# Eight groups of a graph sum sorted by source, and 56 of its chunks summed inside the stage before it

## The chip, the core and the metric

The kernel runs on one core of a Trainium2 chip. The core has TensorE (PE, with its weight loads PEld), VectorE (DVE), ScalarE (ACT), GpSimd (POOL) and SyncE (SP), each with an instruction stream of its own, and 16 DMA engines. The metric is the device time of one execution in microseconds (us). A profiled execution is a run of its own; its trace is what all rows below come from.

## What is computed

A graph of 6250 nodes with 256 features and 106,250 directed edges (100,000 and one loop for each node), sorted by destination. Four blocks follow one another, each added to x: two sums over the edges with a network (512 wide), an attention over 64 slices for each of 8 heads, a normalised sum over the edges (the third sum), and a mixture of 8 experts with two chosen for each node.

```python
x = x + gin(layernorm(x), edges)          # first and second sum
x = x + slice_attention(layernorm(x))     # "desl" is its last step
h = layernorm(x) @ W                      # the third sum
out = segment_sum(h[src] * (dinv[src] * dinv[dst])[:, None], dst, N) + b
x = x + relu((out - mean) * rsqrt(var + eps) * gamma + beta)
x = x + experts(layernorm(x))
```

The third sum is taken before the product with W, which is the same: rows of layernorm(x) times dinv are written to a table, summed by destination, and multiplied by W afterwards.

## The kernel before

The nodes lie in 49 tiles of 128 rows (`NT`). The edges, in the order of their destinations, lie in chunks of 128; without the loops (`others`) there are 782. A chunk is summed in two steps. A gather on GpSimd's queue (`gather`, L162) fetches the 128 rows of a table that the chunk's sources name: an indirect DMA, 1536 bytes a row, three bf16 parts of 256. Then TensorE multiplies them by a one-hot matrix of the destinations (`multiply`, L183, three matmuls, one for each part) into PSUM. VectorE makes the one-hots, up to nine chunks in one instruction (`Sums.hot`, L227).

The destinations are cut into half-overlapping groups k = 0 to 96, each 128 nodes wide, 64 apart. Group k takes the fixed chunks `start(k)` to `start(k+1)`: twelve for k = 0, then eight each. Whether every chunk's destinations lie in its group's window is computed on the chip; if one doesn't, the sum is made zero and redone in a slow loop (`rest`), whose count `n_rest2` is zero for the inputs used here. `Sums.__call__` runs over the chunks of one tile (two groups): it issues gathers up to 14 messages ahead (the ring of buffers), multiplies chunk by chunk, and lets the caller put other work between (`between`). `add` puts a finished group's sum where it belongs: an even group on its tile, an odd one half on each of two.

The stages, in order:

- The first sum (from about 100 to 1125 us) with the first network behind it. Beside it the list of edges without loops is built (`lists`, L754 to L882): steps of VectorE on a 128-row buffer `big`, one handed out at each call of `between`. It writes sources and destinations to DRAM (`flat`) and reads them back in chunk order into `others.src` and `others.dst`, and it leaves the flag for `rest`.
- The second sum (about 1154 to 2145 us), with the second network and the first half of the attention.
- The small attention core (about 2185 to 2200 us), a chain of small steps on TensorE, VectorE and ScalarE that ends in the matrix `M`.
- The output stage (`desl`, L1313 to L1335, from 2200 us). For groups of four tiles: load the slice weights `swT`, four matmuls a tile with M into `po` (L1325, a PSUM tile for two tiles, four buffers), add to x (L1327), layer norm (`layer_norm`, L353 to L367), split in three bf16 parts (`split`, L372 to L376), write to the table T3 in DRAM (L1335, on ScalarE's queue). The order of instructions in this stage is made by a scheduler, engine by engine.
- `rest` for T3 (L1341), a loop that runs no time here.
- The third sum with the experts (from 2301 us): an order written by hand on all engines but GpSimd. For each tile t: SP loads (`load_ahead`, `load_experts`), the scaled own row is added (L1701), then `sums(t, between, 7)`. The seven calls of `between_products` put in the one-hots of the next tile, a piece of a `choice` chain (two tiles each: product with W, layer norm, gate, places), and pieces of expert blocks. `send` scatters the chosen rows to the experts' regions, also an indirect DMA on GpSimd's queue. A tail combines the experts' results.

Of the kernel before, what the change touches and what calls it, by code (L numbers as in the profile page):

```python
# [9 lines left out]
F32 = mybir.dt.float32  # L10
# [11 lines left out]
def gin_transolver_gcn_moe(ctx: ExitStack, tc: tile.TileContext, a: dict, out: bass.AP):  # L22
# [58 lines left out]
    all_edges, others = Chunks(E), Chunks(E - N)  # L81
    NCH2 = others.n
    QC2 = -(-NCH2 // P)
    assert (E, N) == (106250, 6250) and others.per == 16 and CPT == all_edges.per
# [93 lines left out]

    def multiply(pa, hot, msg, F, start, stop, ones=0):

        for s in (2, 0, 1):
            n = F + ones if s == 2 else F
            ins = nc.tensor.matmul(pa[:, :n], hot, msg[:, s * F:s * F + n], start=(start and s == 2),  # L183
                                   stop=(stop and s == 1))
        return ins

    class Sums:
# [4 lines left out]
        def __init__(self, edges, table, pool, depth, hots, ps, add, ones=0, whole=None, is_whole=lambda k: k % 3 == 1):  # L192
            self.whole, self.whole_at = whole, is_whole
            self.edges, self.start = edges, edges.start
            self.table, self.hots, self.ps, self.add, self.ones = table, hots, ps, add, ones
            W = table.shape[1]
            self.F = W // 3
            self.ring = [pool.tile([P, W + 4 * ones], BF16, name=f"msg{i}") for i in range(depth)]
            self.of = [None] * depth
            self.hotf = None  # L200
            self.n, self.made, self.beside = 0, {}, None
            self.early, self.each = False, None

        def is_whole(self, k):
            return self.whole is not None and self.whole_at(k)

        def message(self, c, k):
            i = c % len(self.ring)
            m, whole = self.ring[i], self.is_whole(k)
# [9 lines left out]
        def hot(self, k, c0):  # L219

            if (k, c0) not in self.made:
                n = min(HOTS, self.start(k + 1) - c0)
                if self.is_whole(k):
# [9 lines left out]
        def __call__(self, t, between=None, times=7):  # L233
# [4 lines left out]
            for k in ks:  # L238
                pa = self.ps.tile([P, 512], F32, name="pa", tag="agg", bufs=2)
                for c in range(self.start(k), self.start(k + 1)):  # L240
                    while self.n < min(c + len(self.ring), self.edges.n):
                        of = next(u for u in range(k, 2 * NT) if self.n < self.start(u + 1))
                        table = self.whole if self.is_whole(of) else self.table
                        ins = gather(self.message(self.n, of)[:, :table.shape[1]], table, self.edges.src[:, self.n:self.n + 1])
                        self.n += 1
                        if self.beside is not None:
                            in_order(ins)
                            self.beside(t)
                    c0 = c - (c - self.start(k)) % HOTS
                    hot, msg, ends = self.hot(k, c0)[:, c - c0, :], self.message(c, k), (c == self.start(k), c == self.start(k + 1) - 1)  # L250
                    if self.is_whole(k):
# [28 lines left out]

    def rest(table, add, n_of, count=None, begin=None, kept=None):


        n = nc.values_load(n_of[0:1, 0:1], min_val=0, max_val=NT)
        W = table.shape[1]
        with tc.tile_pool(name="rest", bufs=1) as w, tc.tile_pool(name="rest_ps", bufs=1, space=PSUM) as ps:
            with tc.For_i(0, n, 1) as t:
# [11 lines left out]
                with tc.For_i(c0, c1, 1) as c:  # L299
# [10 lines left out]
                    nc.vector.tensor_scalar(hot, node, k[:, 4:5], None, op0=OP.is_equal)  # L310
                    pa = ps.tile([P, 512], F32, name="pa")
                    if parts_ is F32:
# [135 lines left out]
    with tc.tile_pool(name="own", bufs=1) as own:  # L448
# [153 lines left out]
        with tc.tile_pool(name="g1w", bufs=1) as wp, \  # L602
# [151 lines left out]
            def lists():  # L754
# [77 lines left out]
                nc.sync.dma_start(flat[0], j_[:, :n])  # L832
                yield
                q, r = divmod(n, P)
                for i in range(2):
# [192 lines left out]
    core = {}  # L1028
    right, befores = ExitStack(), ExitStack()
    early = befores.enter_context(tc.tile_pool(name="pre", bufs=1, side="right"))  # L1030
    with tc.tile_pool(name="attn", bufs=1) as ap_:
        tok = ap_.tile([P, KG, D + 1], F32, name="tok")
# [189 lines left out]


        back = ExitStack()
        bw = back.enter_context(tc.tile_pool(name="desl", bufs=2))
# [86 lines left out]

        with back, tc.tile_pool(name="desl_ps", bufs=2, space=PSUM) as ps:  # L1313
            w = bw
            for ts in groups(4, 5):
                J = len(ts)
                x1 = xr[:, ts[0]:ts[-1] + 1, :]
                swT = w.tile([P, 4, HG], F32, name="swT", bufs=3)
                nc.sync.dma_start(swT[:, :J, :], tiles_of(SW, ts))
                for j0 in range(0, J, 2):  # L1320
                    js = range(j0, min(j0 + 2, J))
                    p = ps.tile([P, 2, D], F32, name="po", tag="mm", bufs=4)
                    for j in js:
# [9 lines left out]
                for _ in split(hr[:, :J], hs[:, :J, :], hs[:, :J, :], nc.vector.tensor_tensor):  # L1333
                    pass
                nc.scalar.dma_start(block(T3, ts), hr[:, :J].rearrange("p j s f -> p j (s f)"))  # L1335
    right.close()
    effs.close()


    nc.vector.tensor_scalar(ln3, ln3, own_times, None, op0=OP.mult)  # L1340
    rest(T3, add_to(lambda t: S3[ds(t, 1)].rearrange("o p f -> p (o f)"), D), n_rest2, kept=kept)  # L1341

    late = ctx.enter_context(ExitStack())
    late.enter_context(tc.manual_schedule(engines={mybir.EngineType.SP, mybir.EngineType.PE,
                                                   mybir.EngineType.Activation, mybir.EngineType.DVE}))
    msgs = late.enter_context(tc.tile_pool(name="g3msg", bufs=1))
    hots = late.enter_context(tc.tile_pool(name="g3hot", bufs=4))
    w = late.enter_context(tc.tile_pool(name="g3", bufs=2))
    ew = late.enter_context(tc.tile_pool(name="g3e", bufs=2))
    wxs = late.enter_context(tc.tile_pool(name="g3x", bufs=1))  # L1350
    ps = late.enter_context(tc.tile_pool(name="g3ps", bufs=2, space=PSUM))
    wx = wxs.tile([P, NE, EW], F32, name="wx")
    def add3(k, pa):
        t = k // 2
        if k % 2 == 0:
            return nc.vector.scalar_tensor_tensor(s3s[t], pa[:, :D], ln3[:, 1, t:t + 1], s3s[t],
                                                  op0=OP.add, op1=OP.add)
# [3 lines left out]
    start = others.start  # L1361
    sums = Sums(others, T3, msgs, 14, hots, ps, add3)
    sent = [[] for _ in parts]
# [178 lines left out]
    def load_experts(t):  # L1542

        for e in range(2 * t, min(2 * t + 2, NE)):
            n = KD * HID
# [124 lines left out]
    def between_products(t, k):  # L1670
        if k in (1, 4) and t + 1 < NT:
            of = 2 * t + 2 + k // 4
            if of <= 2 * NT - 2:
                sums.hot(of, start(of))
        if chains and next(chains[0], chains) is chains:
            chains.pop(0)
# [16 lines left out]
    for i, ts_ in enumerate(parts):  # L1693
        for q in range(0, len(ts_), TG):
            ts = ts_[q:q + TG]
            for t in ts:
                load_ahead(t)
                load_experts(t)
                s = s3s[t]

                nc.vector.scalar_tensor_tensor(s, xr[:, t, :], ln3[:, 0, t:t + 1], s, op0=OP.mult, op1=OP.add)  # L1701
                k = iter(range(SLOTS))
# [52 lines left out]
```

## Time and profile before

| | us |
|---|---|
| median of 10 runs (lowest, highest) | 3571.91 (3571.21, 3573.78) |
| profiled run, its own time | 3574.07 |
| its span | 3572.2 |
| POOL busy | 2505.2 (70%) |
| PE busy | 2836.3 (79%) |
| DVE busy | 1548.3 (43%) |
| ACT busy | 866.5 (24%) |

How to read the lines that follow: the slices cut the span into 40 parts of 89 us, and each digit is the busy share in tenths. A group line has the line of code, the engine, the operation, out<-in by the program's names, the count, then busy time and mean ns of one, then the idle time before it and what ended most of that. A timeline line has the start, the duration, engine, line, operation, out<-in, the shape and the count, and in brackets the idle time before and what ended it. "T" is whichever table is read or written, "msg" a message buffer. A matmul in float32 has two records in the trace. The granted clock is the share of TensorE's full speed.

### The profile page before, as it was taken

To read this page: it belongs to the slowest core of one execution; us is meant where nothing else is said; L and a number is where in the kernel's file an instruction comes from. 1 tells how busy PE (TensorE), PEld (TensorE's weight loads), DVE (VectorE), ACT (ScalarE), POOL (GpSimd) and SP (SyncE) were. 2 spreads that over 40 slices of the span, in tenths; PEclk is the share of its full clock that TensorE was granted. 3 is DMA by queue.
4 is the path that set the end of the run, shared out by engine and by line. 5 is a ranking of instruction groups with operands and counts; after the bars stand their busy time and mean duration, and the time that the engine had idled before them with its cause. 6 is when DMAs were issued, how large, how long until landed. Compare 5 with 4: busy or idle time off the path is not lost. (4 is left out here: it accounts for less than half of the span.)

```text
span 3572.2 us, 42390 instructions
## 1 busy us (share of the span) xinstructions
PE 2836.3 (79%) x12790; PEld 1710.9 (48%) x12854; DVE 1548.3 (43%) x3988; ACT 866.5 (24%) x1737; POOL 2505.2 (70%) x2618
## 2 busy tenths in 40 slices
PE   2777788877787899999999988666777777778984
PEld 1334444433345354455444545533555555556653
DVE  5464222222223345554555545634444444444453
ACT  4111111111113022222222223411222232323442
POOL 3787777777775777777777760177777777777765
PEclk6699999999999999999999998866888888889988
DMA  8668888888885999889988883665666666666655
GB/s 272 192 210 258 265 260 260 270 259 255 255 253 196 380 311 307 303 303 311 310 305 303 306 287 101 241 217 172 193 192 192 190 192 191 192 191 208 203 173 171
DMA packets 356497, 861.51 MB, mean 241 GB/s; under 512 B 60104, under 2 KB 158674, under 8 KB 356266
## 3 DMA queue, kind: packets, MB, share of 16 engines
q0 software_dynamic: 174688, 611.60, 55.1%
q1 hardware_dynamic: 175066, 237.50, 19.2%
q10 hardware_dynamic: 6512, 9.63, 0.8%
q8 instruction: 107, 1.75, 0.2%
q14 instruction: 124, 1.02, 0.1%
HBM read 691.29 MB, written 167.21 MB: 240 GB/s over the span
## 5 line engine op out<-in xcount | busy, mean ns | idle before, releaser
L162 POOL DMA_INDIRECT msg<-T,srcT x2059 | 1972.7, 958 | 822.1 <-issue 435.3
L183 PE MATMUL pa<-msg,hot 128*128 128x257 bf16 (+2 forms) x6114 | 1173.8, 318 | 520.1 <-DMA msg<-T,srcT 473.2
L183 PEld LDWEIGHTS <-hot 128*128 128x128 bf16 x6177 | 627.6, 103 | 1180.4 <-issue 881.0
L227 DVE SCALAR_TENSOR_TENSOR hot<-dstT,node 128x1024 bf16<-128x1024 f32 (+2 forms) x255 | 310.4, 1218 | 28.3 <-PE pa L183 16.6
L162 POOL DMA_INDIRECT msg<-T2f,srcT x256 | 242.9, 949 | 78.0 <-issue 30.8
L642 DVE TENSOR_TENSOR dinv<-dinv,pa 128x1 f32<-128x1 f32 x145 | 22.2, 153 | 535.0 <-PE pa L183 499.6
L253 PE MATMUL pa<-msg,hotf 128*128 128x512 f32 x512 | 244.2, 599 | 8.1 <-DMA msg<-T2f,srcT 7.6
L1585 PE MATMUL ph<-wx,xdT 128*128 x448 | 214.1, 600 | 11.1 <-DVE yd L1600 7.1
L1599 PE MATMUL py<-wx,hT 128*128 x896 | 213.6, 381 | 1.1 <-ACT hT L1594 1.1
L919 PE MATMUL p<-h1T,W1b 128*128 128x512 f32 (+2 forms) x480 | 208.7, 533 | 0.0
L928 PE MATMUL p<-W2a,h2T 128*128 128x512 f32 x392 | 206.7, 616 | 0.0
L1599 PEld LDWEIGHTS py<-wx,hT 128*128 128x128 f32 x896 | 168.7, 190 | 65.4 <-issue 42.8
L271 DVE SCALAR_TENSOR_TENSOR s<-s,own,pa 128x512 f32<-128x512 f32 x97 | 71.9, 741 | 183.0 <-PE pa L183 116.8
L1594 ACT ACTIVATE hT<-pt,wb 128x128 f32<-128x128 f32 x448 | 127.7, 368 | 44.7 <-PE pt L1591 42.4
L253 PEld LDWEIGHTS pa<-msg,hotf 128*128 128x128 f32 x512 | 91.3, 190 | 90.7 <-issue 53.4
L1359 DVE TENSOR_TENSOR s<-s,pa 64x256 f32<-64x256 f32 x96 | 40.2, 419 | 214.3 <-PE pa L183 212.8
L1472 POOL DMA_INDIRECT XD<-xn,place x98 | 97.6, 996 | 44.2 <-issue 31.1
L1600 DVE TENSOR_TENSOR yd<-py,wb 128x256 f32<-128x256 f32 x112 | 47.2, 422 | 182.4 <-PE py L1599 178.2
L162 POOL DMA_INDIRECT g<-XD,place x98 | 97.2, 992 | 40.9 <-issue 14.0
L389 ACT ACTIVATE sT<-pt 128x512 f32<-128x512 f32 (+1 forms) x25 | 14.7, 589 | 456.7 <-PE pt L387 456.7
L162 POOL DMA_INDIRECT msg<-T1f,srcT x80 | 85.6, 1071 | 56.0 <-DVE b1b L158 31.9
L1587 ACT ACTIVATE h<-ph 128x512 f32<-128x512 f32 x112 | 66.9, 597 | 217.0 <-PE ph L1585 217.0
(379 smaller groups left out, 3658.6 us busy)
## 6 DMA issues: line engine op xcount, KB each, us to landing
XD<-zeros SPq DMA_DIRECT2D x204, 256.0 KB
msg<-T,srcT POOLq DMA_INDIRECT x2059
T<-tp SPq DMA_DIRECT2D x49, 384.0 KB
wb<-WB SPq DMA_DIRECT2D x112, 130.0 KB
xd<-XD SPq DMA_DIRECT2D x112, 128.0 KB
XD<-yd SPq DMA_DIRECT2D x112, 128.0 KB
T2f<-tf SPq DMA_DIRECT2D x49, 256.0 KB
s<-T2f SPq DMA_DIRECT2D x23, 512.0 KB
```

Of the source, the lines that this page charges most:

```text
L162: return nc.gpsimd.indirect_dma_start(out=msg, out_offset=None, in_=table, in_offset=bass.IndirectOffsetOnAxis(ap=ix, axis=0))
L183: ins = nc.tensor.matmul(pa[:, :n], hot, msg[:, s * F:s * F + n], start=(start and s == 2), stop=(stop and s == 1))
L227: nc.vector.scalar_tensor_tensor(hot[:, :n, :], self.edges.dst[:, c0:c0 + n, None].to_broadcast([P, n, P]), float(k * HALF), node2[:, k % ...
L253: self.last = nc.tensor.matmul(pa[:, :n], hot, msg[:, :n], start=ends[0], stop=ends[1])
L271: return nc.vector.scalar_tensor_tensor(at, at, times[rows], pa[rows, :F], op0=OP.mult, op1=OP.add)
L919: nc.tensor.matmul(p[:, :T], W1b[:, k, m * P:(m + 1) * P], h1T[:, k, :T], start=(k == 0), stop=(k == KH - 1))
L928: nc.tensor.matmul(p, h2T[:, k, j * P:(j + 1) * P], W2a[:, k, :], start=(k == 0), stop=(k == KH - 1))
L1472: ins = nc.gpsimd.indirect_dma_start(out=XD[i], out_offset=bass.IndirectOffsetOnAxis(ap=place[:r, t, c:c + 1], axis=0), in_=xn[:r, j, :], ...
L1585: nc.tensor.matmul(p[:, :HID], xdT[:, k, :], W1[:, k, :], start=(k == 0), stop=(k == KD - 1))
L1587: nc.scalar.activation(h, p[:, :HID], AF.Copy)
L1594: nc.scalar.activation(hT[:, m, :], pt[:, m * P:(m + 1) * P], AF.Relu, bias=b1[:, m:m + 1])
L1599: nc.tensor.matmul(p[:, :D], hT[:, m, :], W2[:, m, :], start=(m == 0), stop=(m == KH - 1))
```

## The change

Eight groups (`EARLY`) are prepared. For each of the groups k = 0 to 7, its last eight chunks (`PER`; 1024 edges) are sorted by source on the chip, so that the first of the eight chunks names only rows at the front of the table T3, the second only rows further on, and so on. `LIMITS` says how many tiles of T3 each of the first seven may need: 12, 16, 24, 32, 36, 44, 46. The order of the edges inside a group does not matter to the sum.

- The sort is put into `lists`: after `flat` is written, rows of 1024 edges for the eight groups are read back onto 8 partitions, source and destination are packed in one number, 55 steps of a merging network of three VectorE instructions each order it, and the numbers are unpacked and written back. Edges out of the window or over a limit raise the flag for `rest`.
- The output stage now holds the third sum's buffers (messages, one-hots, PSUM). After the write of the group of four tiles that completes a limit, eight gathers are issued that read only the rows of T3 so far; after the next group's T3 write in program order their products are made, into sums `begun` in four PSUM banks. The buffers of `po` go from four to three. Eight one-hots (`look`) are made for it, 128 x 1024 each.
- The third sum leaves these 56 chunks out (`left`) and adds the eight begun sums at tile 0. The chains of `choice` begin at tile 4 instead of 2, and the experts' weights are loaded one tile later.
- The attention's pool goes to the other side of the memory, and `rest` takes a PSUM buffer from the stage's own pool.

The scheduler's order in the build of the changed kernel, on TensorE in the output stage: 90 output matmuls (L1325 before), 8 chunk products with 4 output matmuls between them, 11, 8 products with 4 between, 24, 8 with 4, 30, 8 with 4, 13, 8 with 4, 8, and then 16 products. On VectorE the eight one-hots stand between the steps of the attention core: one before and one after the first reciprocal, one after the four scalings of `tok`, one before the copy of `meanT`, two before that of `tokT`, one before that of `kT`, one before the maximum.

```diff
+    PER = others.per // 2
+    EARLY, ALIKE = 8, PER * P
+    LIMITS = [12, 16, 24, 32, 36, 44, 46]
+    def early_chunk(k, j):
+        return others.start(k + 1) - PER + j
...
+        def first_come(self, chunks):
+            self.ahead = {c: None for c in chunks}
+            self.order = chunks + [c for c in range(self.edges.n) if c not in self.ahead]
...
+        def left(self, k):
+            return [c for c in range(self.start(k), self.start(k + 1)) if c not in self.ahead]
...
+        def fetch_next(self, rows=None):
+            c = self.order[self.n]
...
+            ins = gather(self.message(c, of)[:, :table.shape[1]], table[:rows] if rows else table, self.edges.src[:, c:c + 1])
+            self.n += 1
...
+                nc.sync.dma_start(kd, rows_at(1))
+                nc.sync.dma_start(ks, rows_at(0))
...
+                nc.vector.scalar_tensor_tensor(key, ks, float(P), kd, op0=OP.mult, op1=OP.add)
+                m = 1
+                while m < ALIKE:
+                    k = m
+                    while k:
+                        yield
+                        if k == m:
+                            v = key.rearrange("r (b s t k) -> r b s t k", s=1, t=2, k=k)
+                        else:
+                            v = key.rearrange("r (b m) -> r b m", m=2 * m)[:, :, k:2 * m - k]
+                            v = v.rearrange("r b (s t k) -> r b s t k", t=2, k=k)
+                        lo_, hi_ = v[:, :, :, 0, :], v[:, :, :, 1, :]
...
+                        nc.vector.tensor_tensor(less, lo_, hi_, op=OP.min)
+                        nc.vector.tensor_tensor(hi_, lo_, hi_, op=OP.max)
+                        nc.vector.tensor_copy(lo_, less)
+                        k //= 2
+                    m *= 2
...
+                nc.sync.dma_start(rows_at(1), kd)
...
+                nc.sync.dma_start(rows_at(0), ks)
...
+        sums = Sums(others, T3, msgs, 14, hots, ps, None)
+        sums.first_come([early_chunk(k, j) for j in range(PER - 1) for k in range(EARLY)])
+        begun = [ps.tile([P, 512], F32, name="pa", tag=tag, bufs=2) for tag in ("agg", "agg", "tr", "tr")]
+        begun = [t[:, u * D:(u + 1) * D] for t in begun for u in range(2)]
...
+            def look(k):
+                hot_of[k] = w.tile([P, PER, P], BF16, name="ehot", bufs=EARLY)
+                c = early_chunk(k, 0)
+                nc.vector.scalar_tensor_tensor(
+                    hot_of[k], others.dst[:, c:c + PER, None].to_broadcast([P, PER, P]), float(k * HALF),
+                    node2[:, k % 2, None, :].to_broadcast([P, PER, P]), op0=OP.subtract, op1=OP.is_equal)
+            def products(n):
+                for k, j in to_add[:n]:
+                    ins = multiply(begun[k], hot_of[k][:, j, :], sums.message(early_chunk(k, j), k), D, j == 0 and k % 2 == 0,
+                                   j == PER - 2 and k % 2 == 1, after=heads.get((k - 1, j)) if k % 2 else None)
...
             for ts in groups(4, 5):
+                for k in range(EARLY):
+                    if ts[0] // 2 == k // 2 * 2:
+                        look(k)
...
-                    p = ps.tile([P, 2, D], F32, name="po", tag="mm", bufs=4)
+                    p = ps.tile([P, 2, D], F32, name="po", tag="mm", bufs=3)
...
                 nc.scalar.dma_start(block(T3, ts), hr[:, :J].rearrange("p j s f -> p j (s f)"))
+                products(len(to_add))
+                for j, limit in enumerate(LIMITS):
+                    if limit == ts[-1] + 1:
+                        for k in range(EARLY):
+                            sums.fetch_next(limit * P)
+                            to_add.append((k, j))
+            products(len(to_add))
...
-        if chains and next(chains[0], chains) is chains:
+        if t >= EARLY // 2 and chains and next(chains[0], chains) is chains:
...
-                load_experts(t)
-                s = s3s[t]
-                nc.vector.scalar_tensor_tensor(s, xr[:, t, :], ln3[:, 0, t:t + 1], s, op0=OP.mult, op1=OP.add)
+                load_experts(t - 1)
+                for u in range(EARLY // 2 + 1) if t == 0 else [t] if t > EARLY // 2 else []:
+                    nc.vector.scalar_tensor_tensor(s3s[u], xr[:, u, :], ln3[:, 0, u:u + 1], s3s[u], op0=OP.mult, op1=OP.add)
+                for u in range(EARLY) if t == 0 else []:
+                    add3(u, begun[u], True)
```

## The prediction

> **What bounds the kernel now.** I read the page's slices first, then busy time by stretches, then the waits, then the order of time around the change. GpSimd (POOL) is busy in every slice but two, around 2140 to 2320 us:
>
> ```profile
> POOL 3787777777775777777777760177777777777765
> L162 POOL DMA_INDIRECT msg<-T,srcT x2059 | 1972.7, 958 | 822.1 <-issue 435.3
> ```
>
> One gather holds POOL for 0.95 us and the next begins 0.30 us later: a pitch of 1.25. The stretches (length; then busy time and count of PE, PEld, DVE, ACT, POOL; granted clock, DMA share, GB/s) show 160 of them in 200 us of the third sum, with nothing between them, and 81 in 100 us of the first sum. The stage between them has none, and there PE is busy all of the time:
>
> ```profile
> 500.00:600.00 100.00, 79.95 (x370) 40.64 (x369) 27.03 (x49) 16.61 (x28) 75.62 (x81) 0.95 0.85 265
> ...
> 2201.00:2285.00 84.00, 84.00 (x390) 73.71 (x388) 64.85 (x171) 46.76 (x78) 0.00 (x0) 1.00 0.59 201
> ...
> 2320.00:2340.00 20.00, 13.92 (x57) 7.48 (x57) 5.60 (x9) 0.00 (x0) 15.12 (x16) 0.50 0.97 333
> ...
> 2600.00:2800.00 200.00, 151.99 (x861) 111.67 (x860) 93.58 (x357) 58.02 (x140) 151.55 (x160) 0.88 0.64 189
> ```
>
> From 2300 us on, POOL's own waits for TensorE never exceed its issue gap (137 waits, the longest 0.3 us):
>
> ```profile
> POOL msg L162 <- PE pa L183: 41.7, 137, 0.3
> ```
>
> So the first and third sums go at POOL's pitch, and the output stage between 2200.2 and 2298.3 us goes at PE's. Its end is the timeline to look at: the last write of T3, then a point that every engine passes (SP, which needs nothing of T3, starts its loads just then), then the first gather:
>
> ```profile
> 2298.29 0.33 ACTq L1335 DMA_DIRECT2D T<-hr  x1
> 2300.58 2.25 SPq L1376 DMA_DIRECT2D s<-S  x5
> 2301.37 0.94 POOL L162 DMA_INDIRECT msg<-T,srcT  x1 [161.44 <-issue]
> ```
>
> **Taken away after 2301 us.** 56 gathers leave a saturated queue: 56 x 1.25 = 70.0 us. Their 168 matmuls and eight one-hot instructions (1.22 us each, L227) lay beside POOL and give nothing. At the restart VectorE now has five scalings (0.55, L1701), eight additions of begun sums (0.43 to 0.87) and one hot before the first product, some 9 us behind SP's loads; the message ring of 14 covers 14 x 1.25 = 17.5 us, so I charge nothing. Without that cover it would be those 9. The first sends to the experts stand 38 gathers after the restart instead of 66, but as many behind their own tiles as before. SP's s3 load for tile 7 now waits for the first chain at tile 4, and the last four experts' loads queue behind it; no block needs them yet.
>
> **Core stage.** The build puts the eight one-hots of `look` into VectorE's queue between the steps of the small attention, a chain of VectorE and TensorE with waits of 0.3 to 1.9 us (the row of tokT: 1.94 idle before). Laying 1.22 us in each place: two ahead of the reciprocals and their product cost 2.4; one before meanT 0.99 beyond its wait, of which 0.5 shows because ScalarE makes the other half; two before tokT 0.5; one before kT 0.5; one before the maximum 0.3 to 0.4; the third one hides behind prow. M is ready 4.7 us later (bounds 2.4 to 9.8), at 2204.9.
>
> **Output stage, walked in the build's order.** An output matmul is 0.432 us (84.0 us for 390 half records, two each). TensorE's queue now reads: 90 output matmuls, eight chunk products (3 x 0.108 each) with four output matmuls between; 11, batch 2; 24, batch 3; 30, batch 4; 13, batch 5; 8, then batches 6 and 7 together. TensorE is in order, so a product that waits for its message holds every output matmul behind it, and through those VectorE's additions, ScalarE's layer norms, the T3 writes and the next batch's gathers.
> Prices: from a group's last matmul to its T3 write 11.4 to 14 us (2220.9 to 2232.4, 2227.9 to 2241.9); a 768 KB write lands 3.7 after its issue (bytes seen moving until 3.2 after 2284.45, and 0.5 for the semaphore); gather to product 3.2 to 3.9 after 3385.86, up to 6.9 at 2304 with DMA share 0.97; I take 3.9.
> Batch 1 in full: T3's third group was issued at 2232.4, now 2237.1; landed and first gather 2241.0; first message 2244.9; the eighth 8.75 later, 2253.7. TensorE arrives at 2204.9 + 90 x 0.432 = 2243.8 and leaves at 2254.0, where its own work (8 x 0.32 + 4 x 0.43) would have let it go at 2248.1. The further batches the same way, each first gather by the later of T3's write and POOL being free: 2251.0, 2271.4, 2294.0, 2305.7, 2327.6, 2337.6. The last gather is at 2346.4, its product ends at 2350.6, and the restart follows at about 2351.5, 50.1 after 2301.4. The same walk over the old order meets the old T3 writes within 1 us.
> To this I add 2.5 for gathers held by VectorE's two 1.2 us subtractions per group (L373, L376; see the next part), and 4 for the clock: with TensorE busy about half of a stretch the rows above grant 0.50, so some matmuls after a batch run at 0.86. I count nine or ten of them (bounds 0 to 46, all 106 behind batch 1). Restart: +56.6, with bounds 43 (messages 3.2, writes 3.3, full clock) and 80 (messages 6, some 35 matmuls at half clock).
>
> **The sort, in the first sum.** 55 merge steps of three VectorE instructions on 8 x up to 512 elements: 24,063 pairs over 55 is 437 a step. By L1327 (0.69 at 512, 0.42 at 256) min and max take 0.61 each; the copy lies between 0.24 and 0.61, I take 0.40. That is 89 us on an engine that is 27% busy there, in some 26 groups of 10.6 us; hots are made one group ahead, so PE has them. But the list building already in this stage shows what such instructions do to POOL:
>
> ```profile
> 232.93 1.22 DVE L814 TENSOR_TENSOR big<-big 128x1038 int32<-128x1038 int32 x1
> 233.08 1.90 POOL L162 DMA_INDIRECT msg<-T,srcT  x1 [0.30 <-issue]
> 234.68 1.22 DVE L816 TENSOR_TENSOR big<-big 128x1038 int32<-128x1038 int32 x1
> 235.28 1.44 POOL L162 DMA_INDIRECT msg<-T,srcT  x1 [0.30 <-issue]
> ```
>
> A gather that begins during one lasts until it ends, and then its 0.95. From 200 to 300 us the gathers carry 12.7 us beyond 0.95 each, beside 25 such instructions of 1.23 and eight of 0.70. An instruction of length d that a gather meets every 1.25 us costs d x d / 2.5: 25 x 0.605 + 8 x 0.196 = 16.7, of which 0.76 was seen. For the sort: 110 x 0.149 + 55 x 0.064, and 3 for the wide steps around it, is 23; x 0.76 = 17 us. Ends: 4 (the pitch of 1.25 slips past runs of equal instructions, as it does at 223 to 226) and 28. Nothing hides it, since POOL never waits in this stage. SP's two small stores wait for the sort; T2's writes and the zero fills behind them have slack.
> The Trainium skill ("SBUF — State Buffer", Who interferes with whom) lets a copy or tensor_scalar in a two-port mode block GpSimd's descriptor writing, but says that a probe of tensor_tensor stalled no DMA. The rows above show a tensor_tensor doing so. By the page only the 55 copies would count, 55 x 0.064 = 3.5, and the sum would come out near -10 instead of +4.
>
> **Sum.** -70.0 + 56.6 + 17 = +3.6 on the profiled run's own 3574.07 us (span 3572.2; the median of the ten is 3571.91): 3577.7, and with the 2 us between that run and the median 3576. No change, in short: what POOL is spared at the end is spent before the restart and in the sort. 0.2%, 7.1 us, is about what a measurement here can tell from none.
>
> **Rivals.**
> *The batches fit (faster).* Messages in 3.2, writes in 3.3, full clock, sort at 4 to 8: -70 + 44 + 6 = -20, 3553. For it: DMA is only 0.59 busy in that stage, and the gathers' pitch slips past runs of VectorE. Against: batches are spaced by T3 writes, 11 to 14 us behind PE, whatever the messages do.
> *The clock falls (slower).* One place, TensorE after each waiting batch: 0.43 more for each output matmul at half clock. Without any, the sum is -0.4; it passes +7.1 from 18 of the 106 on. With 55 of them it is +23, 3597. For it: 0.50 granted at 2320 to 2340, where PE is busy 70%. Against: output matmuls come in runs of 11 to 30, and 1.00 is granted in them now. The Trainium skill ("TensorE: Matmul & The Clock Gate", The HAM clock gate) has half rate after an idle window of about 3.4 us and full rate after a busy one; by it each of four batches costs up to 3.4 us of half speed, an estimate of 7.
> *It doesn't do what it says.* If a limit on the sorted sources failed, T3's sum would be redone in a loop and milliseconds added. In the reference's inputs the highest source tiles of the seven positions are 6, 14, 20, 26, 32, 37 and 43, each below its limit.
>
> **How the numbers follow.** Balance 0.50 (3563 to 3590: faster 0.06, same 0.26, slower 0.18); batches fit 0.22 (faster 0.19, same 0.03); clock falls 0.27 (slower 0.27); not as said 0.01. Together faster 0.25, same 0.29, slower 0.46. The likeliest is the balance, 3576. The range reaches into both others: 3551 to 3606.
>
> **What would show it.** Gathers in the third sum at 1.25 apart and 56 fewer; the restart at 2301 + 17 + 57 = 2375; PE waiting some 42 us for messages before it; POOL's excess in the first sum up by 17 while the sort runs. It would be wrong if POOL waits for PE in the third sum, or if the sort makes PE late by more than the ring holds.

## The result, and the profile after

| | kernel before | changed kernel |
|---|---|---|
| median of the runs | 3571.71 us (28 runs, 3567.0 to 3573.8) | 3587.35 us (8 runs, 3584.6 to 3595.2) |
| ratio | 1 | 1.0048, 95% interval 1.0040 to 1.0057 |
| the profiled execution: time, span | 3574.07, 3572.2 us | 3585.75, 3583.2 us |

The change makes the kernel 15.6 us slower by the medians (0.44%; the ratio in the table, 1.0048, is the one on record), and 11.0 us by the spans of the two profiled executions, against which everything below is added up.

The page of the changed kernel has the same look: GpSimd busy in all slices but two, and the gathers as many as before, 14 us dearer in sum.

```profile
POOL 3777776777776677777777770367777777777766
L168 POOL DMA_INDIRECT msg<-T,srcT x2059 | 1986.6, 965 | 821.6 <-issue 275.7
```

The stretches that answer to those shown of before (length; busy time and count of PE, PEld, DVE, ACT, POOL; granted clock, DMA share, GB/s). The second runs from the first output matmul to the end of the last one:

```profile
500.00:600.00 100.00, 73.60 (x296) 38.66 (x296) 36.74 (x79) 13.03 (x22) 69.64 (x70) 0.78 0.73 228
...
2227.40:2355.50 128.10, 109.41 (x512) 88.89 (x513) 68.11 (x180) 50.82 (x83) 41.54 (x40) 0.91 0.61 199
...
2600.00:2800.00 200.00, 156.95 (x872) 114.64 (x871) 91.52 (x350) 63.90 (x153) 151.54 (x160) 0.88 0.65 192
```

Read against before: the third sum has the same 160 gathers in 200 us, so it is still bound by GpSimd at 1.25 us each. In the first sum, 11 gathers of 81 are missing from one stretch of 100 us. The output matmuls took 84.9 us with TensorE busy all the time; now they take 128.1, of which TensorE works 109.4.

The end of the stage, from GpSimd's timeline (start, length, and idle time before with what ended it): the last batch but one begins at 2361.39, four gathers of the third sum follow the last batch, and then comes the point that every engine passes.

```profile
2361.39 1.01 POOL L168 DMA_INDIRECT msg<-T,srcT  x1 [13.54 <-SPq L325]
...
2385.34 0.95 POOL L168 DMA_INDIRECT msg<-T,srcT  x1 [0.30 <-issue]
2390.10 0.94 POOL L168 DMA_INDIRECT msg<-T,srcT  x1 [3.82 <-issue]
```

Taking those four off (4 x 1.25), the third sum restarts at 2385.1, 83.7 us later than before (2301.4). The whole difference, read from the starts of the same instructions in both traces:

| | predicted | measured |
|---|---|---|
| up to the last addition to tok (the sort) | +17 | +20.3 (2184.78 to 2205.04) |
| core, from there to the first output matmul | +4.7 | +6.9 (15.45 to 22.34) |
| output stage, from there to the restart | +51.9 | +56.6 (101.1 to 157.7) |
| third sum, restart to last message | -70.0 | -70.9 (1098.5 to 1027.6) |
| from the last message to the end | 0 | -1.8 (172.3 to 170.5) |
| sum | +3.6 | +11.0 |

### The profile page after: what moved, and what is told of

Read it like the earlier page. It is cut to its first block, busy times and chain, and to the rows that moved or that the text cites. A ratio compares the mean times of both kernels' runs of the same rounds, so it can differ in the third digit from the quotient of the medians.

```text
span 3583.2 us, 42612 instructions
## 1 busy us (share of the span) xinstructions
PE 2830.2 (79%) x12790; PEld 1710.9 (48%) x12854; DVE 1651.9 (46%) x4200; ACT 866.7 (24%) x1737; POOL 2518.5 (70%) x2618
## 5 line engine op out<-in xcount | busy, mean ns | idle before, releaser
L189 PE MATMUL pa<-msg,hot 128*128 128x257 bf16 (+2 forms) x5946 | 1128.3, 315 | 487.2 <-DMA msg<-T,srcT 465.0
L189 PEld LDWEIGHTS <-hot 128*128 128x128 bf16 x6009 | 604.9, 102 | 1113.5 <-issue 809.5
L264 DVE SCALAR_TENSOR_TENSOR hot<-dstT,node 128x1024 bf16<-128x1024 f32 (+4 forms) x255 | 302.6, 1188 | 30.0 <-PE pa L189 18.5
L1730 PE MATMUL ph<-wx,xdT 128*128 x448 | 216.1, 605 | 10.6 <-DVE yd L1745 5.2
L168 POOL DMA_INDIRECT g<-XD,place x98 | 97.5, 995 | 38.9 <-issue 15.5
L1730 PEld LDWEIGHTS ph<-wx,xdT 128*128 128x128 f32 x448 | 79.0, 193 | 71.5 <-issue 54.8
```

Of the source, the lines that this page charges most:

```text
L168: return nc.gpsimd.indirect_dma_start(out=msg, out_offset=None, in_=table, in_offset=bass.IndirectOffsetOnAxis(ap=ix, axis=0))
L264: nc.vector.scalar_tensor_tensor(hot[:, :n, :], self.edges.dst[:, c0:c0 + n, None].to_broadcast([P, n, P]), float(k * HALF), node2[:, k % ...
L1730: nc.tensor.matmul(p[:, :HID], xdT[:, k, :], W1[:, k, :], start=(k == 0), stop=(k == KD - 1))
```

## The experiments

The runs ask four things: what the sort costs and why, what holds up the output stage, what the core lost, and whether a mended version wins. The first four runs were on one chip. The other eight ran on two other chips, on which the kernel before takes 4178.9 us (e5 to e8) and 4220.9 us (e9 to e12); each number is therefore compared only with the kernel before on its own chip. The ratios are those on record; they can differ by a few hundredths of a per cent from the quotient of the two medians.

| run | median | kernel before there | ratio (95%) |
|---|---|---|---|
| e1 sort alone | 3594.22 | 3571.77 | 1.0067 (1.0051 to 1.0084) |
| e2 sort alone, thinned | 3582.91 | 3571.77 | 1.0031 (1.0019 to 1.0044) |
| e3 no compare steps | 3571.01 | 3571.77 | 1.0004 (0.9995 to 1.0014) |
| e4 products later | 3560.25 | 3571.77 | 0.9968 (0.9956 to 0.9979) |
| e5 products later, sort thinned | 4142.14 | 4178.86 | 0.9913 (0.9886 to 0.9940) |
| e6 e5 and the core mended | 4144.88 | 4178.86 | 0.9919 (0.9887 to 0.9951) |
| e7 sort with one operand | 4179.12 | 4178.86 | 0.9997 (0.9976 to 1.0017) |
| e8 sort, copies on ScalarE | 4180.58 | 4178.86 | 1.0012 (0.9990 to 1.0034) |
| e9 the kernel of e5 | 4187.66 | 4220.87 | 0.9927 (0.9909 to 0.9945) |
| e10 the kernel of e6 | 4182.69 | 4220.87 | 0.9911 (0.9895 to 0.9928) |
| e11 the kernel of e7 | 4227.56 | 4220.87 | 1.0012 (1.0002 to 1.0023) |
| e12 e10, earlier limits | 4178.18 | 4220.87 | 0.9891 (0.9876 to 0.9907) |

**e1 and e2: the sort alone.** To the kernel before, e1 adds the sort's block of the diff as it stands, and nothing else. e2 spreads the same instructions over twice the turns:

```diff
                     while k:
-                        yield
+                        for _ in range(2):
+                            yield
```

> The kernel before with the sort alone added to its lists; nothing is gathered early. Theory: the sort costs what stage 2 began later in the changed kernel, +21 us (3593): about 10.5 us of gathers held up while VectorE compares, and one wait of about 10 us of GpSimd near 600 us, because some 23 us of TensorE's layer work stands in one piece between two multiplications of one message and the ring of 15 messages covers only 15 x 1.25 = 18.8 us. Rival, as predicted: held gathers alone, +17 (3589), and no wait of GpSimd over 1 us in the first sum. Second rival: the sort is hidden, 3572.

> As the run before it, but each compare step of the sort waits for two turns in place of one, so that the same instructions lie over twice the time. Theory: no such piece is formed on TensorE, GpSimd's wait near 600 us is gone, the held gathers stay: +11 us (3583). Rival: all of the sort's cost is held gathers, the same instructions hold the same gathers: +17 to +21 (3589 to 3593).

e1 costs 22.5 us, e2 11.1. So half of the sort's price is not the sort's own work: the same instructions, thinner, cost half. What goes is a wait, which e1 has as the changed kernel does (10.6 us). GpSimd's waits for TensorE between 300 and 800 us (total, times, longest), in the kernel before, in the changed kernel, in e1 and then in e2:

```profile
POOL msg L162 <- PE pa L183: 28.6, 94, 0.3
```

```profile
POOL msg L168 <- PE pa L189: 44.1, 111, 10.6
```

```profile
POOL msg L168 <- PE pa L189: 45.6, 116, 10.6
```

```profile
POOL msg L168 <- PE pa L189: 29.9, 98, 0.3
```

The changed kernel's timeline of TensorE around that wait, with GpSimd's row behind it:

```profile
576.27 1.09 PE L1012 MATMUL pt<-ident,xs 128*128 128x128 f32 x4
...
578.23 0.38 PE L189 MATMUL pa<-msg,hot 128*128 128x256 bf16 x1
578.44 7.03 PE L1019 MATMUL p<-h0T,W1a 128*128 128x512 f32 x16
...
588.58 12.26 PE L1029 MATMUL p<-h1T,W1b 128*128 128x512 f32 x24
600.68 0.60 PE L189 MATMUL pa<-msg,hot 128*128 128x256 bf16 x4
```

```profile
601.22 0.94 POOL L168 DMA_INDIRECT msg<-T,srcT  x1 [10.57 <-PE pa L189]
```

One message is multiplied in three parts. Between two of them stand 22 us of other matmuls in one piece, 19 of them dense matmuls of the first layer's network. The ring of 15 messages covers 15 x 1.25 = 18.8 us, less what was already used, and GpSimd runs dry for 10.3 us beyond its issue gap. In the kernel before these groups of dense work start every 85 us (438.8, 523.2, 607.7) and lie between the messages; here the group before started at 441.9, so that the next was due near 527. It starts at 576.3, some 50 us late, and the build's order has it in one piece. In e2 the same group is back between the messages, in pairs of records:

```profile
543.65 1.02 PE L988 MATMUL p<-h0T,W1a 128*128 128x512 f32 x2
544.51 0.82 PE L189 MATMUL pa<-msg,hot 128*128 128x257 bf16 x6
545.16 1.02 PE L988 MATMUL p<-h0T,W1a 128*128 128x512 f32 x2
546.03 0.49 PE L189 MATMUL pa<-msg,hot 128*128 128x257 bf16 x3
```

That the piece is formed because the build believes VectorE overloaded is argued from its order, not shown.

The remaining 11 us are held gathers. From 300 to 800 us the gathers carry 13.9 us beyond 0.95 each in the changed kernel, 11.1 in e2, 3.0 in e3, and 1.1 in the kernel before.

**e3: no compare steps.** The loop of compare steps and the test of its result are left out, so that the early chunks are unsorted and cut off at the limits.

```diff
-                m = 1
-                while m < ALIKE:
...
-                nc.vector.tensor_add(row_[:, 2:3], row_[:, 2:3], row_[:, 7:8])
```

> The changed kernel without the 55 compare steps of the sort and without the test of its result; the sort's loads, stores and the limits on the indices stay, the early gathers fetch unsorted edges. Theory: 3587.3 - 21 = 3566 or so, stage 2's first gather back at 1154 to 1156; the rest of the change then gains 5 to 6 us against the kernel before. Rival: the sort costs 17 and the rest gains 1 to 2 us, 3570.

It measured 3571.0, 16.3 under the changed kernel where 21 were expected. Stage 2's first gather is back (1.2 us behind the kernel before), but with these data the output stage takes 162.2 us from first output matmul to restart, 4.5 more than in the changed kernel. So e3, without the compares, gains nothing that can be told from zero (0.8 us, ratio 0.9995 to 1.0014). In it the core and the output stage take 67.9 us more than before (6.8 and 61.1), nearly all of the 70 by themselves; in the changed kernel they take 63.5.

**e4: products later.** The products of a batch are put, in TensorE's order, behind 56 further output matmuls, four at a time; all else is the changed kernel.

```diff
+                    pair[0] += 1
+                    products(4)
+                    fetches()
...
-                products(len(to_add))
                 for j, limit in enumerate(LIMITS):
                     if limit == ts[-1] + 1:
-                        for k in range(EARLY):
-                            sums.fetch_next(limit * P)
-                            to_add.append((k, j))
+                        to_fetch.extend((k, j, limit) for k in range(EARLY))
+                fetches()
```

Here `products` skips what was fetched less than 7 pairs of tiles ago, and `fetches` issues gathers while the ring of 14 has room.

> The changed kernel with the early products placed later in TensorE's order: those of a batch not before 7 pairs of output tiles (56 output matmuls, 24 us) have passed since its group, four at a time. Theory: TensorE waits for messages and then runs at half clock, which makes its last output matmul 30 us later than the products themselves need (18.7 waiting, 11.5 slow); without that the last output matmul moves from 2355 to about 2328, the restart from 2385 to 2352-2355, the total to 3555-3558. Rival: the ring of 14 messages then holds GpSimd back instead, or the chain from a group's last matmul to its written rows bounds the stage, and the restart moves by less than 10 us: 3578-3587.

3560.25: 27.1 us under the changed kernel and 0.32% under the kernel before, though 2 to 5 us over what was expected. From first output matmul to restart it takes 132.0 us in place of 157.7. The same stretch as above, first output matmul to end of the last, in e4:

```profile
2231.40:2331.70 100.30, 96.02 (x478) 83.35 (x479) 67.14 (x177) 50.19 (x82) 39.32 (x37) 0.98 0.74 244
```

100.3 us where the changed kernel needs 128.1. TensorE's waits for messages in it, first in the changed kernel and then in e4:

```profile
PE pa L189 <- DMA msg<-T,srcT: 18.5, 14, 3.8
```

```profile
PE pa L189 <- DMA msg<-T,srcT: 4.3, 2, 3.2
```

The 196 output matmuls need 84.9 us (before), and a chunk's product 3 x 0.108 = 0.32. The changed kernel puts 40 products ahead of its last output matmul: 13.0 us. So of its 43.2 us more, 18.5 are waiting, 13.0 are work, and the remaining 11.7 are the same work at a lower clock (0.91 over the stretch). In e4 28 products are 9.1 us, 4.3 are waiting, 2.0 the clock (0.98). The clock loss goes with the waits. GpSimd shows the same thing from the other side, in its starts after a wait in the changed kernel, and then in e4:

```profile
2302.05 0.94 POOL L168 DMA_INDIRECT msg<-T,srcT  x1 [15.32 <-DMA T<-hr]
...
2325.64 0.94 POOL L168 DMA_INDIRECT msg<-T,srcT  x1 [13.32 <-PE po L1465]
...
2337.48 0.94 POOL L168 DMA_INDIRECT msg<-T,srcT  x1 [1.42 <-DMA T<-hr]
...
2361.39 1.01 POOL L168 DMA_INDIRECT msg<-T,srcT  x1 [13.54 <-SPq L325]
```

```profile
2283.37 0.94 POOL L168 DMA_INDIRECT msg<-T,srcT  x1 [2.60 <-DMA T<-hr]
...
2298.98 1.61 POOL L168 DMA_INDIRECT msg<-T,srcT  x1 [5.22 <-DMA T<-hr]
...
2314.85 0.94 POOL L168 DMA_INDIRECT msg<-T,srcT  x1 [4.90 <-DMA T<-hr]
...
2339.90 1.01 POOL L168 DMA_INDIRECT msg<-T,srcT  x1 [2.57 <-SPq L325]
```

43.6 us of standing idle between batches have become 15.3. The rival, that the ring of 14 would hold GpSimd back instead, falls.

**e5 and e9: both mended.** e4 with the thinned sort of e2; e9 is the same kernel again.

> e4 (products 7 pairs later) with the sort thinned as in e2. Theory: the two costs lie in different stages and add up: 3560.25 - (3594.22 - 3582.91) = 3549, GpSimd's wait of 11 us near 600 us gone. Rival: what is won in the first sum is lost to waits further on: 3553 or more.

> The kernel of e5 once more, on a chip that runs the kernel before in about 3572 us. Theory: the two costs add up, 3560.25 - 11.3 = 3549, 23 us under the kernel before. Rival: what the thin sort wins is lost further on, 3553 or more. Should the chip be one where gathers wait for the transfers, as in e5 to e8, then 30 to 40 us under the kernel before, as there.

On their chips it is 36.7 and 33.2 us faster than the kernel before. The 3549 us expected could not be tested: no chip of these two runs the kernel before in 3572. There gathers begin on average 1.46 us apart in the first sum (206 from 800 to 1100 us in e9, against 241 in e4), because GpSimd waits between some of them, and TensorE's granted clock in that stretch is 0.83 against 0.96 in e4. So GpSimd has slack there, and a sort costs little: e8 below, the whole thinned sort with only its copies moved to ScalarE, is 1.7 us over the kernel before on e5's chip (1.0012, 0.9990 to 1.0034). Nearly all of e5's gain is then that of the early gathers with their products placed later.

**e6 and e10: the core.** Two edits to e5: `rec` is placed in the pool of `tok`, and the one-hots may not stand ahead of M in VectorE's order.

```diff
+        rec = ap_.tile([P, 2, KG], F32, name="rec")
...
-            rec = w.tile([P, 2, KG], F32, name="rec")
...
+                tc.add_manual_dep(ins.ins, made_M.ins.name, ...)
```

> e5 with two edits in the core: rec lies in the pool of tok, and the eight one-hots of the early chunks stand behind the last VectorE step of M in VectorE's order. Theory: the core is late by 6.9 us, 3.4 of it the wait of rec for the transfer of swT and 3.3 the one-hots in VectorE's queue; both go, the first output matmul stands 22.8 us behind the last addition to tok as in the kernel before (2184.36 and 0.42 to 2200.23 there is 15.5; 22.3 in the changed kernel), and the total falls 5 to 7 us under e5. Rival: 8 x 1.2 us of one-hots then delay the additions of the first output groups by as much, and the total is that of e5 within 2 us.

> The kernel of e6 once more. In e6 the core came 7.1 us earlier, and the stretch from first to last output matmul was 3.4 us longer than in e5. Theory: 3 to 5 us under e9, 3544 to 3546. Rival: the last early gathers and the ring set the restart, not the core: that of e9 within 1.5 us.

(The 22.8 in the expectation of e6 is a slip: the kernel before has 15.5, as its bracket says.) In the changed kernel VectorE's timeline shows what the core met, a wait and then one-hots between the steps:

```profile
2204.62 0.42 DVE L1306 TENSOR_TENSOR tok<-tok,ptok 128x257 f32<-128x257 f32 x1 [0.43 <-PE ptok L1304]
2208.44 0.17 DVE L1352 TENSOR_SCALAR rec<-tok 128x4 f32<-128x4 f32 x1 [3.40 <-DMA SW<-swT]
2208.84 1.22 DVE L1441 SCALAR_TENSOR_TENSOR ehot<-dstT,node 128x1024 bf16<-128x1024 f32 x1 [0.23 <-issue]
2209.98 0.17 DVE L1353 RECIPROCAL rec<-rec 128x4 f32<-128x4 f32 x1
```

`rec` takes up a place that stage 2's last store of SW still reads, because the change opens the ring's pool ahead of the core and everything moves. In e6 the wait is gone:

```profile
2515.97 0.42 DVE L1308 TENSOR_TENSOR tok<-tok,ptok 128x257 f32<-128x257 f32 x1 [0.43 <-PE ptok L1306]
2516.43 0.17 DVE L1353 TENSOR_SCALAR rec<-tok 128x4 f32<-128x4 f32 x1
```

From the end of that addition to the first output matmul it is 15.45 us in e6 (2516.39 to 2531.84), as in the kernel before, against 22.3. But the one-hots are then in the way of VectorE's part of the first output groups: the first early gather comes 41.9 us behind the first output matmul in e6 and 38.3 in e5 (41.8 in e10, 38.0 in e9), and first to last output matmul takes 104.7 us in e6 and 101.4 in e5, 107.0 in e10 and 100.4 in e9. So 3.3 to 6.5 of the 6.9 won are given back, and the times agree: e6 is 2.7 us over e5, e10 5.0 under e9, neither beyond their spread. The mechanism is shown, the gain isn't.

**e7, e11 and e8: what holds a gather.** All on the base of e2. In e7 and e11 each minimum and maximum takes a constant in place of its second operand; the limits on the indices and the test are left out and the lists stay unsorted. In e8 the copy is on ScalarE.

```diff
-                        nc.vector.tensor_tensor(less, lo_, hi_, op=OP.min)
-                        nc.vector.tensor_tensor(hi_, lo_, hi_, op=OP.max)
+                        nc.vector.tensor_scalar(less, lo_, 1e30, None, op0=OP.min)
+                        nc.vector.tensor_scalar(hi_, hi_, -1e30, None, op0=OP.max)
```

```diff
-                        nc.vector.tensor_copy(lo_, less)
+                        on_act(lo_, less)
```

> e2 with the minimum and maximum of each compare step taken against a constant in place of the other half, so that every instruction reads one operand from SBUF; shapes, count and places stay, the limits on the indices and the test are left out, and the lists stay unsorted, which the rest of this kernel does not need. Theory: it is reading two operands that holds the gathers, the 110 minima and maxima stop doing so, 3572 to 3576. Rival: any VectorE instruction of this length holds a gather as often: 3580 to 3583.

> The kernel of e7 once more; e7 ran where GpSimd had slack, so that its time says nothing of held gathers, though their sum in the trace, 9.8 us, was that of the two-operand steps of e5, 10.2. Theory after e7: any VectorE instruction on SBUF in f32 of this length holds gathers; the excess stays at 9 to 11 us and the time at 3580 to 3583. Rival, as predicted: two operands hold, 3572 to 3576.

> e2 with the copy of each compare step on ScalarE in place of VectorE. Theory: the copies read one operand and hold nothing, 3581 to 3584, no change. Rival: they hold gathers as the two others do, a third of 11 us goes: 3579. Second rival: only copies hold gathers: 3573 to 3575.

The times say little, since GpSimd has slack on those chips. The traces do say something: for each gather between 310 and 820 us (800 in e2, e7 and e8) I took the VectorE instruction that overlaps its first 0.95 us most, and counted the gathers that lasted over 1.0 us:

```
overlapped by                  e2 (two operands)  e9 (two)     e7 (one)     e11 (one)    e8 (no copy)
minimum, maximum, copy         22 of 73           22 of 67     22 of 44     22 of 43     32 of 67
a one-hot (bf16 out, 1.2 us)    1 of 57            2 of 40      3 of 42      0 of 42      0 of 40
```

One operand holds as two do; min and max without copies do as well. What hardly holds is the one-hot, which is the longest of them and reads two operands (dstT and node). So "reads two operands from SBUF" is the wrong line. In the same five traces none of the 794 gathers that no VectorE instruction overlapped was held, and of those under the first layer's two subtractions (p, tp; 128x512, 0.69 us) 14 of 157 were. e11's 1.0012 (1.0002 to 1.0023) gives no sign of a gain either. The edit of e7 and e11 also changed a second thing: minimum and maximum took 0.43 and 0.39 us on average there, 0.62 and 0.61 in e2, on the same shapes. That the shorter ones hold for a reason of their own is not excluded, and which property of an instruction decides was not found.

**e12: earlier limits.** e10 with the limits 8, 16, 24, 28, 36, 40, 44.

> The kernel of e6 with the limits 8, 16, 24, 28, 36, 40, 44 in place of 12, 16, 24, 32, 36, 44, 46: four of the seven batches may be gathered a group earlier, and the sorted edges of this case still fit (their largest sources lie at tiles 6.4, 14.2, 20.2, 26.5, 32.1, 37.7 and 43.4). Theory: GpSimd stood idle 15 us between its first early gather and the last in e4; with batches earlier by 7 us most of that goes: 5 to 10 us under e10. Rival: the ring of 14 and products 24 us behind their groups hold the gathers back: that of e10 within 2 us.

4178.18, 4.5 us under e10 where 5 to 10 were expected, and 1.09% under the kernel before by the ratio: the best of the runs, though its interval and e10's overlap. The first gather behind the common point, in e10 and then in e12:

```profile
2693.62 0.94 POOL L168 DMA_INDIRECT msg<-T,srcT  x1 [5.23 <-issue]
```

```profile
2680.30 0.95 POOL L168 DMA_INDIRECT msg<-T,srcT  x1 [4.43 <-issue]
```

From the last addition to tok it takes 153.6 us in e12, against 167.4 in e10. In e10 four gathers of the third sum stand ahead of that point and in e12 none, so that like with like the restart is 8.8 us earlier (162.4 to 153.6).

## Why the prediction was right, and where it was not

The forecast was 3576, no change to speak of, from a balance of -70.0, +56.6 and +17. The kernel came out at 3587.35, slower by 15.6, inside the range of 3551 to 3606 and inside the balance's own range of 3563 to 3590. "No change" it is not: 15.6 is over the 7.1 that the prediction took as the least that can be told from none, and "slower" had 0.46 in all. The picture was right: what GpSimd is spared at the end is spent before the restart and in the sort. The three costs were each too low, by 3.3, 2.2 and 4.7; the gain was right. That the misses stayed this small is in part luck, for inside the sort and inside the output stage errors of 4 to 10 us in opposite directions cancelled, as the next paragraphs show.

*Taken away, -70.0:* -70.9. POOL never waits for PE there (all gaps at 0.30 from 2390 on); the ring did cover the additions at the restart.

*The sort, +17:* +20.3, and for another reason. The step that failed is "hots are made one group ahead, so PE has them" and "Nothing hides it, since POOL never waits in this stage". The hots did come in time, but TensorE's dense work did not keep its places, and the wait that followed cost 10.3 us. The held gathers, priced at 17, were 11 (e2) to 12.8 (13.9 less 1.1). Together that is 23, of which 20.3 were left at the last addition to tok. The named way to be wrong, "if the sort makes PE late by more than the ring holds", is what happened; it had no price in the sum. In the prediction's own rows a held gather ends 0.83 and 0.82 us behind the instruction that held it (234.15 to 234.98, 235.90 to 236.72), not 0.95. The reading with which e7 began, that two operands in SBUF are what holds, falls with e7, e11 and the one-hots. The measured rows against the Trainium skill ("SBUF — State Buffer", Who interferes with whom) stand where the page says that a probe of tensor_tensor stalled no DMA: a tensor_tensor does hold a gather, by e8 without any copy, 32 times of 67. The prediction left out that the same section also has a tensor_tensor with both inputs in SBUF contend with GpSimd's reads, so that its "only the 55 copies" goes further than the page.

*The core, +4.7:* +6.9. The one-hots cost 3.5 (6.9 less 3.4), less than priced (the pieces that the prediction lists add up to 4.3, not 4.7); the wait of 3.4 for stage 2's store was not seen. The prediction walked VectorE's queue, but not what a moved pool makes an instruction wait for.

*The output stage, +51.9 behind the core:* +56.6. The walk gave the batches' first gathers 36, 46, 67, 89, 101, 123 and 133 us after M; they came at 38, 49, 75, 98, 110, 134 and 144. PE's waits for messages were 18.5 us before its last output matmul and 16.3 after it, 34.8 together, where 42 were predicted:

```profile
PE pa L189 <- DMA msg<-T,srcT: 16.3, 13, 9.0
```

The clock took 11.7 where 4 were (and 7 by the estimate from the skill's page); the row of before behind the 4 has TensorE busy 70% at 0.50, not about half. So the waiting was over-sized by 7 and the clock under-sized by 8. The way from a T3 write to its gather was under-sized as well: where a batch waited for nothing else, its first gather came 5.7 and 4.7 us behind the issue of the write (2296.39 to 2302.05, 2332.78 to 2337.48), not 3.7. The last bytes of these two writes moved until 4.5 and 3.6 after the issue, and the gather began 1.1 behind them; the 0.5 that the prediction put there for the semaphore is in no run. The rest is the common point: GpSimd idles 3.5 us there with gathers at hand, where the walk had the restart 0.9 us behind the last product.

*Rivals.* "The clock falls" was priced at 0.43 for each matmul at half speed, with the sum passing +7.1 from 18 on; 11.7 us are 27 of them. The outcome lies between the balance and this rival, on the rival's side of the bound, though the clock alone did not put it there: the shorter waits took back as much. "The batches fit" was wrong about this kernel and right about what was missing: with products that meet their messages, e4 stands at -11.5, 0.9968.

## What to carry to other kernels

A product put into an in-order engine's queue before its data can be there stops everything queued behind it; count the way from the producer's last instruction through store, gather and message (here 24 us, 56 output matmuls, which left 4.3 of the 18.5 us of waiting) and place the consumer that far behind, instead of directly behind the next group. Extra work on an engine that is idle enough can still displace other work in the order of a third engine: after such a change, look for the longest stretch of that order without the operation that frees the ring, and hold it against the ring's cover. When pools move, look at which new store or load the first instruction of the next stage now waits for.

## What the runs showed of the hardware

- A VectorE minimum, maximum or copy on 8 partitions of f32, 0.27 to 0.75 us long, lengthened 30 to 51% of the gathers that it overlapped most, with one operand as with two; a one-hot of 1.2 us on 128 partitions with a bf16 result 3% (6 of 221), and no VectorE instruction none (0 of 794).
- In the output stage the clock was granted in full (1.00) while TensorE was never idle, 0.98 with 4.3 us of waits in 100, and 0.91 with 18.5 in 128.
- The same kernel before takes 3572, 4179 and 4221 us on three chips. In the runs traced on the slower two the gathers of the first sum are on average 1.46 us apart in place of 1.25, since GpSimd waits between some of them, though one gather still takes 0.94 to 0.95 us; TensorE's granted clock in the same stretch is 0.83 in place of 0.96. Why the chips differ stays open.
